# Graph attention with heads: exponentials and turnings run one chunk further ahead in tiles 5 to 23

## The chip, the cores and the metric

The kernel runs on one core of a Trainium2 chip. The core has five engines that run their own instruction streams and wait for each other by semaphores: TensorE (PE in the profile, with its weight loads as PEld), VectorE (DVE), ScalarE (ACT), GpSimd (POOL) and SyncE (SP), which in this kernel issues most of the DMA transfers. The metric is the device time of one execution in microseconds (us): the median of three runs for the kernel before, 2910.59 us.

## The reference

A network of two layers over 3327 nodes with 256 features. Layer 0 is a graph convolution and a mixture of 8 experts, layer 1 a graph attention and a block of four attention heads. The change lies in that last block alone, in the profile the stage from about 960 us to the end. Cut to it:

```python
sx = einsum('bsh,ndh->bnsd', layernorm(x), hl_w) + hl_b      # 4 heads of 64
q = einsum('bnsd,neod->bneso', sx, wq)                        # 4 query experts per head
k, v = einsum(sx, wk), einsum(sx, wv)
scores = einsum('bnesd,bntd->bnest', q, k) * 8 + causal
qkv = where(sx == 0, 0, softmax(scores) @ v)
gs = softmax(gate(qkv)); mixed = sum over the experts of qkv * gs
hn = layernorm(mixed + resid)                                 # resid from sx
out = x + gated(layernorm(fc2(relu(fc1(hn))) + hn))
```

So there are 3327 x 3327 causal scores for each of 16 pairs of head and query expert, each row with its own maximum, exponentials and sum, and then a weighted sum of values.

## The kernel before

Nodes are cut in 26 tiles of 128 rows. The method `heads` works through units, one for each tile t and head h, and cuts each unit's causal row of t + 1 key tiles into t // 4 + 1 chunks g of three or four key tiles (up to 512 columns). There are 392 chunks in all, 312 of them in tiles 5 to 23 (4 heads x 78). What happens to a chunk:

- `fill`: TensorE computes the scores of four query experts into four buffers of PSUM (pqk, 512 columns each), which are all that the pool `ps` has; other products use them too.
- `drain`: VectorE copies each of the four into SBUF (sc, one of nine buffers) and takes the row maximum on the way; the last chunk of a unit adds the causal mask, and then the maxima of the unit's chunks are reduced to anmax.
- `weigh`: ScalarE takes the exponentials in place, one instruction for each query expert, and their sums into aden. It needs anmax, so the unit must be fully drained.
- `turn`: VectorE transposes 32 x 32 blocks of sc in place.
- `values`: SyncE issues four transfers that bring the chunk's values into vr (three buffers).
- `attend`: TensorE multiplies the turned weights with vr into po, which collects over the chunks of a unit.

At a unit's end `over` takes po into ot times the mask sxd (ScalarE copies, GpSimd multiplies, from tile 5 on), and one step later `back` turns it with ptO into qkv. The generator `prepare` makes the projections of the next tile (psxt, pv, pk, pq) a part at a time, and `tail` mixes, normalises, applies the two linear layers and stores a finished tile; `run` advances them by one part, and `quiet` issues small exponentials that were put off.

The loop at the end of `heads` (from line 1493) sets the order of all of this by hand, and `InOrder` (lines 47 to 93) makes every engine keep the order in which its instructions are issued. Nearly all instructions therefore have line 61 in the profile, so groups are told apart by their tiles. One pass of the loop is a step. In step k the order was: drain as far as `wanted(k)`, value sums of chunk k, turning of chunk k + 1, value transfers and two exponentials of chunk k + 2, back and over where a unit has ended, parts of prepare and tail, the other exponentials of chunk k + 2, and the scores of one more chunk:

```python
drain_to(wanted(k))
attend(u, g)
if k + 1 < len(chunks):
    turn(*chunks[k + 1])
if ahead:                       # chunk k + 2
    values(*ahead)
    if ahead[1]:
        weigh(*ahead, range(2))
```

`wanted(k)` is k + 3 + t // 4 with t the tile of chunk k + 2: enough that the unit of that chunk is drained. In tiles 20 to 23 that keeps eight of the nine sc buffers in use, in tiles 24 and 25 all nine.

In tile 0 to 4 the queries of a tile (qts) lie in an sc buffer as well. `prepare` names its normalised features xn and its nonzero mask nz by one tag with one buffer, so the next tile's xn takes the buffer of this tile's nz. In tiles 0 to 4 two tiles can be in preparation at a time, four parts apart; later one is.

Of the kernel before, what the change touches and what calls it, by code (L numbers as in the profile page):

```python
# [12 lines left out]
F32 = mybir.dt.float32  # L13
# [9 lines left out]
P = 128  # L23
# [78 lines left out]
class Net:  # L102
# [753 lines left out]
    def heads(self, xs, vs, out):  # L856
        tc, a = self.tc, self.a
        nc = InOrder(tc)
        Q = 32
        with ExitStack() as ctx:  # L860
# [4 lines left out]
            tl = ctx.enter_context(tc.tile_pool(name="att", bufs=2))  # L865
            sm = ctx.enter_context(tc.tile_pool(name="atsm", bufs=4))
# [8 lines left out]


            load = dict(act=0.0, dve=0.0)
            lazy = deque()

            def empty(dst, src, n, scale=None):  # L880
                if load["act"] + 0.14 + 0.00086 * n <= load["dve"] + 0.1 + 0.00112 * n:
# [26 lines left out]
            def prepare(t, res):  # L908
# [43 lines left out]
                nz = self.work.tile([P, 2, P], F32, tag="xn", name="nz", bufs=1)  # L952
# [1 line left out]
                load["act"] += 0.6  # L954
                yield

                sxd = self.work.tile([P, 4, P], F32, tag="sxd", name="sxd", bufs=3)
                for k in range(2):
                    for s in range(2):
                        nc.sync.dma_start(  # L960
                            out=sxd[ds(64 * k, 64), s::2, :], in_=nz[ds(64 * s, 64), :, :]
                        )
                pp = ps.tile([P, 4, 64], F32, tag="b", name="pv")
                for c in range(2):
                    nc.tensor.matmul(
# [3 lines left out]
                empty(v, pp, D)  # L969
                yield  # L970

                pp = [ps.tile([P, 2, P], F32, tag="b", name="pk") for _ in range(2)]
                for c in range(2):
                    for s in range(2):
                        r = ds(64 * s, 64)
# [5 lines left out]
                for b in range(4):  # L981
                    nc.sync.dma_start(
                        out=vs[:, :, 4 * t + b, :].rearrange("h r d -> r h d"),
                        in_=v[ds(Q * b, Q), :, :],
# [9 lines left out]
                for c in range(2):  # L994
                    for i in range(2):
                        for s in range(2):
                            r = ds(64 * s, 64)
# [11 lines left out]
            def quiet():  # L1009

                while lazy:
                    lazy.popleft()()

            def run(gens):

                gens[:] = [g for g in gens if next(g, None) is None and g.gi_frame is not None]

            tails, preps, ready = [], [], {}
# [12 lines left out]
            def span(t, g):  # L1031


                n = t // 4 + 1
                lo, hi = (t + 1) * g // n, (t + 1) * (g + 1) // n
                return lo, hi - lo
# [42 lines left out]
            def weigh(u, g, experts):  # L1079

                n = span(u["t"], g)[1] * P
                q = ready[u["t"]]
                if u["h"] == g == 0 and 0 in experts:
                    q["den"] = sm.tile([P, 16, 7], F32, tag="den", name="aden", bufs=2)
                for k in experts:
                    e = u["sc"][g][:, k, :n]
                    nc.scalar.activation(
                        e, e, AF.Exp, bias=u["nmax"][:, k : k + 1],
                        accum_out=q["den"][:, 4 * u["h"] + k, g : g + 1],
                    )  # L1090
                    load["act"] += 0.26 + 0.00088 * n

            def values(u, g):

                lo, n = (4 * i for i in span(u["t"], g))
                v = u["v", g] = vrp.tile([P, 16, 64], F32, tag="vr", name="vr")
                for q in range(4):
                    nc.sync.dma_start(out=v[ds(Q * q, Q), :n, :], in_=vs[u["h"], :, lo : lo + n, :])

            def turn(u, g):  # L1100


                n = span(u["t"], g)[1] * P
                w = u["sc"][g][:, :, :n]
                nc.vector.transpose(w, w)
                load["dve"] += 0.1 + 0.00417 * n
# [7 lines left out]
            def attend(u, g):  # L1114


                t = u["t"]
                w, v = u["sc"][g], u["v", g]
                lo, n = (4 * i for i in span(t, g))
                for b2 in range(0, n, 2):  # L1120
                    for k in range(2):
                        for q in range(4):
                            r, b = ds(Q * q, Q), b2 + k

                            after = 4 * t + q - lo
                            if b > after and t:
                                continue
                            nc.tensor.matmul(
                                po[ds(64 * k, 64), q, :, :], v[r, b, :], w[r, :, ts(b, Q)],
                                start=(g == b2 == 0), stop=(b + 2 > after if t else b2 == 2),  # L1130
                            )

            def over(u):

                u["ot"] = tl.tile([P, 4, P], F32, tag="ot", name="ot", bufs=1)
                to = u["ot"].rearrange("p e (q i) -> p q e i", q=4)
                there = u["sxd"][:, u["h"] : u["h"] + 1, :]
                if u["t"] < 5 or u is units[-1]:

                    nc.vector.tensor_tensor(  # L1140
                        to, po,
                        there.rearrange("p o (q i) -> p q o i", q=4).to_broadcast([P, 4, 4, Q]),
                        ALU.mult,
                    )
                    load["dve"] += 0.7
                else:
                    nc.scalar.copy(to, po)
                    nc.gpsimd.tensor_tensor(
                        u["ot"], u["ot"], there.to_broadcast([P, 4, P]), ALU.mult
                    )  # L1150
                    load["act"] += 0.6
# [108 lines left out]
            def tail(t, sx, qkv, glp, den):  # L1260
# [35 lines left out]
                nz = tl.tile([P, 2, D], F32, tag="nzf", name="nzf", bufs=1)  # L1296
# [17 lines left out]
                fo = tl.tile([P, D], F32, tag="fo", name="fo", bufs=3)  # L1314
# [10 lines left out]
                fot = tl.tile([P, 2, P], F32, tag="fxt", name="fot", bufs=2)  # L1325
# [8 lines left out]
                f3 = fo.rearrange("p (h d) -> p h d", h=4)  # L1334
                nc.gpsimd.tensor_tensor(f3, f3, fg.unsqueeze(2).to_broadcast([P, 4, 64]), ALU.mult)
                nc.gpsimd.tensor_tensor(fo, fo, x, ALU.add)
                nc.sync.dma_start(out=out[ts(t, P), :], in_=fo)

            def last_tail(t, c, sx, r):

# [3 lines left out]
                if c == 0:  # L1344
                    r["fx"] = tl.tile([P, D], F32, tag="fx", name="fx", bufs=3)
                    r["fo"] = tl.tile([P, D], F32, tag="fo", name="fo", bufs=3)
                    r["fot"] = tl.tile([P, 2, P], F32, tag="fotl", name="fotl", bufs=1)
                else:
                    x = r["x"] = tl.tile([P, D], F32, tag="xend", name="xend", bufs=1)
                    nc.sync.dma_start(out=x, in_=xs[ts(t, P), :])  # L1350
                fx, fo, fot = r["fx"][:, half], r["fo"][:, half], r["fot"][:, c, :]
# [79 lines left out]
                fo, fot, x = r["fo"], r["fot"], r["x"]  # L1431
# [10 lines left out]
            chunks = [(u, g) for u in units for g in range(u["t"] // 4 + 1)]  # L1442
# [19 lines left out]
            def fill_next():  # L1462
                nonlocal filled
                if filled < len(chunks):
                    u, g = chunks[filled]
                    if g == 0:
                        begin(u)
                    fill(u, g)
                    filled += 1

            def drain_to(n):
                nonlocal drained
                while drained < min(n, len(chunks)):
                    if filled == drained:
                        fill_next()
                    drain(*chunks[drained])
                    drained += 1

            def wanted(k):

                return k + 3 + chunks[min(k + 2, len(chunks) - 1)][0]["t"] // 4

# [2 lines left out]
            for k in range(2):  # L1487
                values(*chunks[k])
                weigh(*chunks[k], range(4))
            turn(*chunks[0])  # L1490
            fill_next()
            ended = None
            for k, (u, g) in enumerate(chunks):
                ahead = chunks[k + 2] if k + 2 < len(chunks) else None
                drain_to(wanted(k))
                attend(u, g)
                if k + 1 < len(chunks):
                    turn(*chunks[k + 1])
                if ahead:
                    values(*ahead)  # L1500
                    if ahead[1]:
                        weigh(*ahead, range(2))
                if ended:
                    back(ended)
                last = u if g == u["t"] // 4 else None
                if last:
                    over(u)
                if not ended or u["t"] < 8:
                    run(preps)
                    run(tails)  # L1510
                ended = last
                if ahead:
                    weigh(*ahead, range(2 if ahead[1] else 0, 4))
                quiet()
                if filled == drained:
                    fill_next()
            back(ended)
            while tails:
                run(tails)
                quiet()  # L1520

# [552 lines left out]
```

## Time and profile before

| what | us |
|---|---|
| three runs | 2901.87, 2910.59, 2912.35 |
| the profiled execution: time, span | 2907.43, 2905.6 |
| mean granted TensorE clock over the span | 0.973 |
| busy: TensorE, VectorE, ScalarE, GpSimd | 2643.7, 2376.5, 1790.9, 1075.2 |
| turnings of tiles 0 to 4 (24 chunks) | 975 to 1117 |
| turnings of tiles 5 to 23 (312 chunks) | 1117 to 2633 |
| turnings of tiles 24 and 25 (56 chunks) | 2633 to 2876 |

The profile's page has an engine's busy time, the same in 40 equal slices of the span with a digit for tenths, the chain of work that ended last, and the groups of instructions by what they write and read (out<-in). A line of waits reads: the waiting engine and tile, the releasing engine and tile, us in total, times, longest. A row of a table by stretches gives the stretch and its length, then busy us and instructions of PE, PEld, DVE, ACT and POOL, the granted clock, the DMA share and GB/s. A row of a timeline gives the start, the duration, the engine, the operation, and in brackets how long the engine had been idle and what released it. "issue" is time in which an engine waited for nothing that the profile shows. Matmuls are pipelined and their ends are modelled.

### The profile page before, as it was taken

How to read it: one execution, taken by the hardware profiler on the slowest of the kernel's cores; microseconds unless marked ns; L12 is line 12 of the kernel's file. 1: busy time of each engine (PE TensorE's matmuls, PEld its weight loads, DVE VectorE, ACT ScalarE, POOL GpSimd, SP SyncE). 2: the span in 40 equal slices, each digit the busy share in tenths (PEclk: the TensorE clock that was granted, in tenths of full speed). 3: DMA queues.
4: the chain of work that ended last, by engine and by line, in shares of the span. 5: the costliest groups of instructions: out<-in, count | busy, mean ns of one | idle time of the engine just before them, and what ended most of it. 6: DMA issues, size and time to landing. Idle time of an engine off the chain costs nothing.

```text
span 2905.6 us, 125250 instructions
## 1 busy us (share of the span) xinstructions
PE 2643.7 (91%) x53422; PEld 1958.9 (67%) x53422; DVE 2376.5 (82%) x5525; ACT 1790.9 (62%) x5130; POOL 1075.2 (37%) x1562
## 2 busy tenths in 40 slices
PE   7999998779889799999999999999999999999995
PEld 5888888657668676666666666666666666556654
DVE  5203643689999597899999999999999999999996
ACT  6410145555545367777777776777667777677774
POOL 5541634622231148645454332333223222223122
PEclk9999989989999799999999999999999999999998
DMA  9994668647775233433434434343333433434332
GB/s 382 384 324 138 196 225 274 235 152 284 247 250 170 62 90 95 112 103 113 119 102 117 118 113 112 106 116 116 112 112 109 122 117 116 114 116 116 112 111 76
DMA packets 258189, 449.71 MB, mean 155 GB/s; under 512 B 58816, under 2 KB 156608, under 8 KB 257504
## 3 DMA queue, kind: packets, MB, share of 16 engines
q1 hardware_dynamic: 245536, 417.50, 45.9%
q0 software_dynamic: 6576, 18.02, 1.7%
q8 instruction: 421, 6.90, 1.0%
q10 hardware_dynamic: 5520, 6.18, 0.6%
q14 instruction: 136, 1.11, 0.1%
HBM read 393.37 MB, written 25.88 MB: 144 GB/s over the span
## 4 chain that ended last, share of the span: by engine, by line
DVE 34%; PE 28%; issue 3%; ACT 3%; POOL 1%; DMA 1%; SPq 0%; POOLq 0%; DVEq 0%; ACTq 0%
DVE sc L61 31%; PE po L61 11%; PE pqk L61 10%; PE ptO L61 2%; PE acc L61 2%; ACT sc L61 1%; PE psxt L61 1%; PE pq L61 1%; PE ph L61 1%; ACT sq L61 0%; PE pt L61 0%; DVE anmax L61 0%; POOL qkv L61 0%; SPq L61 0%; PE pk L61 0%
## 5 line engine op out<-in xcount | busy, mean ns | idle before, releaser
L61 ACT ACTIVATE sc<-sc,anmax 128x512 f32<-128x512 f32 (+3 forms) x1568 | 1041.4, 669 | 111.7 <-DVE anmax L61 111.7
L61 PEld LDWEIGHTS po<-sc,vr 32*64 32x64 f32 x43728 | 664.9, 131 | 390.6 <-DVE sc L61 232.9
L61 PE MATMUL po<-sc,vr 32*64 32x128 f32 x43728 | 770.6, 276 | 110.3 <-DVE sc L61 62.8
L61 DVE STREAM_TRANSPOSE sc<-sc 128x2048 f32<-128x2048 f32 (+3 forms) x392 | 816.2, 2082 | 10.7 <-ACT sc L61 10.4
L61 PE MATMUL pqk<-kt,qt 64*128 64x512 f32 (+1 forms) x2944 | 729.4, 585 | 14.7 <-DVE fgs L61 5.9
L61 DVE TENSOR_SCALAR_CACHE_REDUCE sc<-pqk 128x512 f32<-128x512 f32 (+2 forms) x1152 | 654.7, 622 | 64.3 <-PE pqk L61 63.0
L61 PEld LDWEIGHTS pqk<-kt,qt 64*128 64x128 f32 x2944 | 290.5, 187 | 224.5 <-issue 107.3
L61 PE MATMUL acc<-wh,p 128*128 128x259 f32 x1352 | 310.0, 387 | 35.0 <-DVE p L61 34.8
L61 PEld LDWEIGHTS acc<-wh,p 128*128 128x128 f32 x1352 | 254.2, 191 | 93.1 <-DVE p L61 52.5
L61 PE MATMUL acc<-y,pan 128*128 128x256 f32 x1352 | 298.2, 382 | 1.7 <-issue 1.7
L61 ACT ACTIVATION_READ_ACCUMULATOR sc<-sc,anmax 128x1 f32 x1568 | 299.3, 191 | 0.0
L61 PEld LDWEIGHTS acc<-y,pan 128*128 128x128 f32 x1352 | 257.1, 191 | 37.9 <-issue 2.5
L61 POOL TENSOR_TENSOR ot<-ot,sxd 128x512 f32<-128x512 f32 x83 | 106.0, 1277 | 474.7 <-ACT ot L61 460.9
L61 DVE CUSTOM_DVE_ANT_0 sc<-pqk,mask 128x512 f32<-128x512 f32 (+3 forms) x416 | 242.2, 637 | 28.6 <-PE pqk L61 27.7
L61 ACT ACTIVATE u<-u,d 128x512 f32<-128x512 f32 (+1 forms) x182 | 125.2, 688 | 159.8 <-DVE u L61 159.7
L61 DVE SCALAR_TENSOR_TENSOR u<-bc,d 128x512 f32<-128x512 f32 (+1 forms) x182 | 135.7, 746 | 0.1
L61 DVE SCALAR_TENSOR_TENSOR p<-pan,u 128x512 f32<-128x512 f32 (+1 forms) x182 | 126.8, 697 | 10.2 <-PE acc L61 5.8
L61 ACT COPY qkv<-ptO 128x272 f32<-128x272 f32 x104 | 39.7, 382 | 143.9 <-PE ptO L61 143.9
L61 PE MATMUL ptO<-igw,ot 128*128 128x68 f32 x832 | 116.1, 283 | 1.9 <-DVE mx L61 0.8
L61 ACT ACTIVATE junk<-ar 128x1664 bf16<-128x1664 f32 x52 | 82.8, 1592 | 55.7 <-DMA ar<-in_adj_dram 55.2
L61 PEld LDWEIGHTS ptO<-igw,ot 128*128 128x128 f32 x832 | 101.5, 192 | 20.0 <-issue 12.7
L61 DVE CUSTOM_DVE_ANT_0 sg<-sg,dst 128x1664 bf16<-128x1664 bf16 (+2 forms) x56 | 99.7, 1789 | 1.2 <-ACT dst L61 1.0
(356 smaller groups left out, 3086.6 us busy)
## 6 DMA issues: line engine op xcount, KB each, us to landing
vr<-vs SPq DMA_DIRECT2D x976, 128.0 KB
ar<-in_adj_dram SPq DMA_DIRECT2D x104, 832.0 KB
vr<-vs SPq DMA_DIRECT2D x544, 96.0 KB
pan<-in_adjt_dram SPq DMA_DIRECT2D x156, 256.0 KB
pan<-in_adjt_dram SPq DMA_DIRECT2D x26, 1024.0 KB
pan<-in_adjt_dram SPq DMA_DIRECT2D x20, 832.0 KB
w1e<-w SPq DMA_DIRECT2D x59, 256.0 KB
took<-places SPq DMA_DIRECT2D x59, 129.0 KB
```

Of the source, the lines that this page charges most:

```text
L61: made = make(*args, **kw)
```

## The change

The exponentials of a chunk and its turning are issued one step earlier while chunk k belongs to tile 5 or later and chunk k + 3 to tile 23 or earlier (`extra(k)` is then 1): exponentials for chunk k + 3, turning for chunk k + 2, and `wanted(k)` drains one chunk further. Two counters, `flipped` and `weighed`, replace the fixed distances. Value transfers stay two chunks ahead. The two exponentials ahead of `back` and `over` and the rest behind the parts of prepare and tail keep their places in the step.

The store of a finished tile is put in a list, and `quiet` issues it at the end of the second step after it was listed. The four transfers of sxd move behind the value projection, one part of `prepare` later. aden has a third buffer, and fotl of the last tile uses the two buffers of xres in place of its own.

```diff
@@ prepare: the mask transfers after the value projection
+                pp = ps.tile([P, 4, 64], F32, tag="b", name="pv")
+                for c in range(2):
+                    nc.tensor.matmul(
+                        pp[:, 2 * c : 2 * c + 2, :], sxt[:, c, :], wv[:, c, :], start=True, stop=True
+                    )
+                v = self.work.tile([P, 4, 64], F32, tag="v", name="v", bufs=1)
+                empty(v, pp, D)
+                yield
+
                 sxd = self.work.tile([P, 4, P], F32, tag="sxd", name="sxd", bufs=3)
                 for k in range(2):
                     for s in range(2):
                         nc.sync.dma_start(
                             out=sxd[ds(64 * k, 64), s::2, :], in_=nz[ds(64 * s, 64), :, :]
                         )
-                pp = ps.tile([P, 4, 64], F32, tag="b", name="pv")
...
-                empty(v, pp, D)
-                yield
@@ quiet
                 while lazy:
                     lazy.popleft()()
+                for store in stores:
+                    store[0] -= 1
+                while stores and stores[0][0] < 0:
+                    stores.popleft()[1]()
@@ weigh
-                    q["den"] = sm.tile([P, 16, 7], F32, tag="den", name="aden", bufs=2)
+                    q["den"] = sm.tile([P, 16, 7], F32, tag="den", name="aden", bufs=3)
@@ tail
-                nc.sync.dma_start(out=out[ts(t, P), :], in_=fo)
+                stores.append([2, partial(nc.sync.dma_start, out=out[ts(t, P), :], in_=fo)])
@@ last_tail
-                    r["fot"] = tl.tile([P, 2, P], F32, tag="fotl", name="fotl", bufs=1)
+                    r["fot"] = tl.tile([P, 2, P], F32, tag="xres", name="fotl", bufs=2)
@@ the loop
+            def extra(k):
+
+                t = chunks[min(k + 3, len(chunks) - 1)][0]["t"]
+                return int(chunks[k][0]["t"] >= 5 and t // 4 + 1 <= 6)
+
             def wanted(k):
 
-                return k + 3 + chunks[min(k + 2, len(chunks) - 1)][0]["t"] // 4
+                c = min(k + 2 + extra(k), len(chunks) - 1)
+                return k + 3 + extra(k) + chunks[c][0]["t"] // 4
...
-            ended = None
+            ended, flipped, weighed = None, 1, 2
             for k, (u, g) in enumerate(chunks):
-                ahead = chunks[k + 2] if k + 2 < len(chunks) else None
                 drain_to(wanted(k))
                 attend(u, g)
-                if k + 1 < len(chunks):
-                    turn(*chunks[k + 1])
-                if ahead:
-                    values(*ahead)
-                    if ahead[1]:
-                        weigh(*ahead, range(2))
+                while flipped < min(k + 2 + extra(k), weighed, len(chunks)):
+                    turn(*chunks[flipped])
+                    flipped += 1
+                if k + 2 < len(chunks):
+                    values(*chunks[k + 2])
+                rest = []
+                while weighed < min(k + 3 + extra(k), len(chunks)):
+                    c = chunks[weighed]
+                    if c[1]:
+                        weigh(*c, range(2))
+                    rest.append((*c, range(2 if c[1] else 0, 4)))
+                    weighed += 1
                 if ended:
                     back(ended)
...
-                if ahead:
-                    weigh(*ahead, range(2 if ahead[1] else 0, 4))
+                for c in rest:
+                    weigh(*c)
                 quiet()
...
-            while tails:
+            while tails or stores:
                 run(tails)
                 quiet()
```

More of the change, by code (lines that the diff above doesn't have):

```diff
@@ L877, in heads @@
             load = dict(act=0.0, dve=0.0)
-            lazy = deque()
+            lazy, stores = deque(), deque()
             def empty(dst, src, n, scale=None):
@@ L955, in prepare @@
                 yield
[L957 to L962, printed above, removed]
                 pp = ps.tile([P, 4, 64], F32, tag="b", name="pv")
@@ L970, in prepare @@
                 yield
+                sxd = self.work.tile([P, 4, P], F32, tag="sxd", name="sxd", bufs=3)
+                for k in range(2):
+                    for s in range(2):
+                        nc.sync.dma_start(
+                            out=sxd[ds(64 * k, 64), s::2, :], in_=nz[ds(64 * s, 64), :, :]
+                        )
                 pp = [ps.tile([P, 2, P], F32, tag="b", name="pk") for _ in range(2)]
```

## The prediction

> **What bounds the kernel now.** I read the page's parts 1, 2 and 4 first, to see which engines fill the stage that the change touches, then the table by stretches, then the waits of each engine in that stage, and last a timeline of one stall.
>
> ```profile
> PE 2643.7 (91%) x53422; PEld 1958.9 (67%) x53422; DVE 2376.5 (82%) x5525; ACT 1790.9 (62%) x5130; POOL 1075.2 (37%) x1562
> ...
> DVE  5203643689999597899999999999999999999996
> ...
> DVE 34%; PE 28%; issue 3%; ACT 3%; POOL 1%; DMA 1%; SPq 0%; POOLq 0%; DVEq 0%; ACTq 0%
> DVE sc L61 31%; PE po L61 11%; PE pqk L61 10%; PE ptO L61 2%; PE acc L61 2%; ACT sc L61 1%; PE psxt L61 1%; PE pq L61 1%; PE ph L61 1%; ACT sq L61 0%; PE pt L61 0%; DVE anmax L61 0%; POOL qkv L61 0%; SPq L61 0%; PE pk L61 0%
> ```
>
> The 392 turnings (the transposes of sc, in chunk order) date the chunks: tile 5 is turned from 1117 us, tile 24 from 2633 us, and what lies between, 1516 us, is where the change works. Its 312 chunks take 4.86 us each. The table by stretches and the waits of VectorE, TensorE and SyncE's queue, each asked for 1117 to 2633 us (engine <- releaser: us, times, longest):
>
> ```profile
> 1117.00:2633.00 1516.00, 1420.61 (x39861) 968.75 (x39851) 1426.45 (x3205) 1101.89 (x3471) 567.91 (x778) 0.99 0.39 113
> ```
> ```profile
> DVE sc L61 <- PE pqk L61: 74.6, 89, 4.4
> ...
> DVE sc L61 <- ACT sc L61: 1.4, 3, 1.0
> ...
> PE po L61 <- DVE sc L61: 42.9, 61, 1.5
> PE po L61 <- issue: 29.9, 35, 1.8
> ...
> SPq L61 <- PE po L61: 572.6, 247, 6.6
> SPq L61 <- POOL fo L61: 115.0, 20, 8.8
> ...
> SPq L61 <- POOL nz L61: 7.4, 7, 1.3
> ```
>
> VectorE and TensorE are each busy 94% here and take turns on the chain. VectorE idles 89.5 us, 74.6 of them waiting for scores. TensorE idles 95 us, 42.9 of them at the head of a value sum, for the turning. A timeline of both engines shows the two waits as one event:
>
> ```profile
> 1628.44 2.30 DVE L61 STREAM_TRANSPOSE sc<-sc 128x2048 f32<-128x2048 f32 x1
> ...
> 1632.56 1.77 DVE L61 STREAM_TRANSPOSE sc<-sc 128x1536 f32<-128x1536 f32 x1
> 1634.79 0.69 DVE L61 TENSOR_SCALAR_CACHE_REDUCE sc<-pqk 128x512 f32<-128x512 f32 x1 [0.46 <-PE pqk L61]
> ...
> 1627.64 1.65 PE L61 MATMUL pqk<-kt,qt 64*128 64x384 f32 x8
> 1630.80 2.09 PE L61 MATMUL po<-sc,vr 32*64 32x128 f32 x116 [1.51 <-DVE sc L61]
> 1632.82 0.44 PE L61 MATMUL pt<-ident,xn 128*128 128x128 f32 x2
> 1633.09 0.61 PE L61 MATMUL ph<-fc,h 128*128 128x128 f32 x4
> 1633.63 1.99 PE L61 MATMUL pqk<-kt,qt 64*128 64x512 f32 x8
> ```
>
> TensorE stood 1.51 us until the turning of this very chunk ended, then had a value sum, 0.81 us of other work and the next scores to do, and VectorE, through with its second turning, found none and stood 0.46 us. Had the value sum begun 0.46 us sooner, VectorE would not have stood.
>
> **The change, part by part.**
>
> Work per step: nothing added or removed. A chunk keeps four drains (0.61 us apart at 512 columns), one turning (2.24 us), four exponentials and the same matmuls. Draining, exponentials and turning all move one chunk further ahead of the value sum, so their spacing among themselves stays: exponentials one step before their turning, as now. Only the value sum's gate loosens: chunk k was turned one step before, now two.
>
> What that is worth. Removing TensorE's waits gains only where VectorE's stalls follow them. By stretch (1117 to 1363, to 1632, to 1980, to 2289, to 2633 us) VectorE waits for scores 22.0, 10.7, 17.0, 15.4, 9.5 us and TensorE for turnings 1.9, 6.0, 10.5, 9.1, 15.3 us. No stretch can give more than the smaller of its two: 1.9 + 6.0 + 10.5 + 9.1 + 9.5 = 37.0 us. And TensorE cannot save up at will: scores fill four banks, the last of which is free only when the previous drain ends; the second half of a fill (1.0 of 1.99 us) follows, and the turning takes 2.24 us, so a value sum can begin at most some 1.2 us before that turning ends. Going through the stalls in order, crediting each with the TensorE waits since the last one, carrying no more than 1.0 us, gives 16 us; with 1.5 us, 19; the 37 needs no limit. The row nearest to a typical stall (1.51 us waited, 0.46 stalled) is paid in full, so it lies above the 16 and 19; many stalls follow a run in which TensorE is full, so it lies well under the 37. I take 24 us and keep both ends. The first stretch gives almost nothing: TensorE is full there. Late next after that: still the scores, behind TensorE's own extra work (1.1 us of ptO, 1.16 of psxt).
>
> A page of the Trainium skill judges this otherwise. Perfetto Trace Analysis, Identifying the Most-Contended Engine, holds matmul busy time a bad measure of how full TensorE is, and weight-load busy time a good one. By it TensorE, at 968.75 of 1516 us, has a third to spare, and the whole 74.6 us would go; the timeline above, where each matmul group from 1630.80 on starts when the one before is due to end, does not agree.
>
> Entry and exit. At chunk 24 one extra fill and drain stand ahead of the value sum and four more exponentials behind it, at chunk 25 there is a second turning; at chunk 333 there is no drain and no turning. VectorE's total is unchanged; it waits once for the first bank pair of the extra fill (about 1 us, half of 1.99) and once for a value sum at the exit (up to 2.09, or nothing where TensorE has a lead). Bounds 0 to 4 us, I take 2, the middle.
>
> Score buffers: in tiles 20 to 23 all nine instead of eight are live. The new drain needs the buffer of the value sum before last, and its scores come after that sum in TensorE's order, so it waits no longer than for its scores. Cover: tiles 24 and 25 run with nine now, and VectorE waits for scores only 3.5 us from 2633 to 2758 us. Cost 0.
>
> Stores: 22 here, 0.357 us of issue each, unchanged in number. Now SyncE's queue stands 115.0 us behind POOL's last addition into fo, with the four vr transfers of the next chunk behind it, and TensorE waits for those. It waited 4.0 us for vr in all, 8 times. Issued two steps (some 10 us) later the store waits for nothing; fo has three copies, one taken per tile of 43 us or more. Gain 0 to 4 us; I take 1, since the waits seen sit mostly in the shadow of the scores before them.
>
> Mask transfers: four of 0.606 us per tile, past one chunk's vr transfers and value projection, in front of the same vs stores. SyncE loses a 7.4 us wait for POOL's nz. From tile 5 on they are read a tile later. In tiles 1 to 4 the next tile's normalising takes the buffer of nz, so POOL waits for the transfer: 3.8 us, once, now. One step there is 147 us / 24 = 6.1 us, three tiles: 0 to 18 us. VectorE idles 37 of those 147 us, which covers part of it, and the one wait seen is 3.8 us, far from the upper end: I take 1.
>
> The third aden copy and fotl in the xres buffers: no instruction; xres was last loaded a tile earlier. Cost 0.
>
> Sum: -24 + 2 - 1 + 1 = -22 us. The profiled execution took 2907.4 us (span 2905.6 and 1.8 around it), 3.2 us under the median 2910.6; so 2885 us, 0.9% under the median.
>
> **Rivals.**
>
> 1. TensorE is simply full. Its 29.9 us of issue gaps and its back-to-back groups stay, stalls are paid a step later, under 10 us is left: about 2902 us. For: the first stretch, 22.0 us of stalls with 1.9 of waits. Against: the last, where the waits exceed the stalls.
>
> 2. Slower, by ScalarE. In tiles 8 to 11 (three chunks a head) the exponentials of a head's first chunk now fall in the step that also copies ptO, and the copy stands ahead of them; ScalarE waited for ptO 36.7 us in 18 waits from 1117 to 1363 us, 2.0 each, up to 4.1. VectorE then stands before the turning. The slack is a turning and a drain less four exponentials: 1.7 + 1.9 - 2.4 = 1.2 us at 384 columns, 1.9 at 512; from a copy later than that on, it decides. Its price is 16 heads by 2.0 us, 32 us, and with the lead eaten up by it the time is 2907.4 + 32 = 2939 us; at half the price, with the gain kept, 2901. Against: tiles 5 to 7 have this order now, and VectorE waits for exponentials 1.4 us in the whole stretch.
>
> 3. VectorE alone bounds it: all 74.6 us go, 2907.4 - 74.6 = 2833 us. For: VectorE's digits of 9 in slices 18 to 39. Against: the stretch sums above. The page named above sides with this one.
>
> **The numbers.** Forecast 0.60, rival 1 0.18, rival 2 0.14, rival 3 0.08. Forecast's own range: -37 - 4 to -16 + 4 + 7, so 2866 to 2902 us. The range of 2855 to 2918 us takes that in with the runs' own spread (2901.9 to 2912.4), all of rival 1 and the mild part of rival 2; beyond it lie most of rival 3 and the rest of rival 2, under 2 in 10. Half a percent, 14.6 us, is about what a measurement of this kernel can tell from no change: under 2896 us counts as faster. That is 0.88 of the forecast and rival 3: 0.61. Slower: rival 2 and a little of the rest, 0.16. Same: 0.23.
>
> **What would show it.** Right: "PE po <- DVE sc" falls from 42.9 us to under 10, "DVE sc <- PE pqk" from 74.6 to about 50; "SPq <- POOL fo" is gone; the turnings of tiles 5 to 23 span about 1494 us; the stretch to 1363 us hardly moves. Rival 1: the first wait falls and the second stays. Rival 2: "DVE sc <- ACT sc" grows from 1.4 us to 15 or more, in tiles 8 to 11. Rival 3: "DVE sc <- PE pqk" falls under 15. I would be wrong if TensorE's waits merely change name (to "PE pqk <- DVE sc", the banks), if its clock drops below the 0.99 of this stretch when it is pressed harder, or if tiles 0 to 4 lengthen beyond 147 us.

## The result and the profile after

| | before | changed |
|---|---|---|
| median, us | 2910.59 (2901.87 to 2913.4) | 2867.09 (2863.63 to 2868.76) |
| profiled execution: span, us | 2905.6 | 2862.2 |
| first turning of the stage, us | 974.8 | 982.1 |
| turnings of tiles 0 to 4, us | 142.2 | 141.8 |
| turnings of tiles 5 to 23, us | 1516.2 | 1468.3 |
| turnings of tiles 24 and 25, us | 242.6 | 240.5 |

The ratio is 0.9848 (95% interval 0.9834 to 0.9863): 1.5% faster, where 0.9% was forecast. The gain lies where the change works: 47.9 us in tiles 5 to 23. The first turning came 7.4 us later in this execution; 7.0 us of that lay ahead of the stage's first projection (psxt), in stages that the change does not touch. The page of the changed kernel, parts 1, 2 and 4:

```profile
PE 2665.0 (93%) x53422; PEld 1979.1 (69%) x53422; DVE 2368.9 (83%) x5525; ACT 1790.0 (63%) x5130; POOL 1075.3 (38%) x1562
...
DVE  5203643589999588899999999999999999999996
...
DVE 35%; PE 28%; ACT 3%; issue 2%; POOL 1%; DMA 0%; SPq 0%; POOLq 0%; DVEq 0%; ACTq 0%
```

The same five engines, tiles 5 to 23 (from 1124 to 2592 us here), in the table by stretches:

```profile
1124.00:2592.30 1468.30, 1443.59 (x39850) 991.73 (x39841) 1420.80 (x3205) 1102.96 (x3474) 568.06 (x779) 1.00 0.40 116
```

The waits of VectorE, TensorE and SyncE's queue in the same stretch (us, times, longest):

```profile
DVE sc L61 <- PE pqk L61: 34.5, 36, 4.5
DVE sc L61 <- ACT sc L61: 0.6, 2, 0.4
...
PE pqk L61 <- DVE sc L61: 4.9, 6, 2.0
PE po L61 <- issue: 2.2, 4, 1.3
...
PEld pqk L61 <- DVE sc L61: 53.8, 201, 2.6
...
SPq L61 <- POOL fo L61: 5.8, 4, 2.6
```

The line "PE po <- DVE sc" (42.9 us before) is gone; a little of it came back as "PE pqk <- DVE sc", the wait for a bank of scores (2.1 before, 4.9 now), and the weight loads of a fill wait longer for a bank ("PEld pqk <- DVE sc", 26.5 us before, 53.8 now). VectorE's wait for scores fell by 40.1 us, from 89 waits to 36. Of the forecast's signs, "SPq <- POOL fo" did not quite go: 5.8 us are left. VectorE is busy 96.8% of the stretch (94.1% before), TensorE 98.3% by its modelled ends. One thing in these lines was not forecast: TensorE's idle time inside the value sums that the profile ascribes to nothing, "PE po <- issue", fell from 29.9 us to 2.2.

The two engines in the timeline of the changed kernel, to be held against the one in the prediction:

```profile
2023.42 2.31 DVE L61 STREAM_TRANSPOSE sc<-sc 128x2048 f32<-128x2048 f32 x1
2025.65 0.65 DVE L61 CUSTOM_DVE_ANT_0 sc<-pqk,mask 128x512 f32<-128x512 f32 x1
...
2022.61 2.32 PE L61 MATMUL pqk<-kt,qt 64*128 64x512 f32 x8
2023.56 0.54 PEld L61 LDWEIGHTS pqk<-kt,qt 64*128 64x128 f32 x4 [0.32 <-DVE sc L61]
2024.86 2.10 PE L61 MATMUL po<-sc,vr 32*64 32x128 f32 x128
2026.89 0.71 PE L61 MATMUL ph<-fxt,fc 128*128 128x128 f32 x4
2027.53 2.05 PE L61 MATMUL pqk<-kt,qt 64*128 64x512 f32 x8
```

The value sum starts at 2024.86 us, 0.79 us before VectorE is through with the turning and takes its next instruction, at 2025.65; under the old order it would have waited for that end. In the whole of tiles 5 to 23 about half of the value sums start before the turning at the place of the old gate ends, by up to 1.46 us; before the change none did. The fill ahead of this one took 2.32 instead of 1.99 us: its second half stood 0.32 us for a bank, in the row of the weight loads (PEld).

### The profile page after: what moved, and what is told of

Same layout as the page of the kernel before. It is cut to its first block, busy times and chain, and to the rows that moved or that the text cites. A ratio compares the mean times of both kernels' runs of the same rounds, so it can differ in the third digit from the quotient of the medians.

```text
span 2862.2 us, 125012 instructions
## 1 busy us (share of the span) xinstructions
PE 2665.0 (93%) x53422; PEld 1979.1 (69%) x53422; DVE 2368.9 (83%) x5525; ACT 1790.0 (63%) x5130; POOL 1075.3 (38%) x1562
## 4 chain that ended last, share of the span: by engine, by line
DVE 35%; PE 28%; ACT 3%; issue 2%; POOL 1%; DMA 0%; SPq 0%; POOLq 0%; DVEq 0%; ACTq 0%
DVE sc L61 32%; PE pqk L61 10%; PE po L61 10%; PE acc L61 2%; ACT sc L61 2%; PE ptO L61 2%; PE psxt L61 1%; PE pt L61 1%; PE pq L61 1%; PE ph L61 0%; ACT sq L61 0%; PE pk L61 0%; PE pv L61 0%; DVE anmax L61 0%; DVE gl L61 0%
## 5 line engine op out<-in xcount | busy, mean ns | idle before, releaser
L61 PE MATMUL po<-sc,vr 32*64 32x128 f32 x43728 | 761.1, 276 | 31.6 <-DVE sc L61 21.5
L61 PE MATMUL pqk<-kt,qt 64*128 64x512 f32 (+1 forms) x2944 | 764.4, 585 | 19.0 <-DVE fgs L61 6.6
L61 PEld LDWEIGHTS pqk<-kt,qt 64*128 64x128 f32 x2944 | 315.9, 185 | 239.5 <-issue 80.9
```

The source lines that it names most:

```text
L61: made = make(*args, **kw)
```

## Experiments

### Which part of the change it is

Theory L: the lead alone is the gain. Theory S: since the issue gaps went too, and SyncE's queue no longer stands behind POOL, the stores are part of it. Three kernels, each with one part:

```diff
 lead_only, against the changed kernel (and sxd back in front of pv)
-                stores.append([2, partial(nc.sync.dma_start, out=out[ts(t, P), :], in_=fo)])
+                nc.sync.dma_start(out=out[ts(t, P), :], in_=fo)
 stores_only (sxd back too), masks_only (store back too)
-                return int(chunks[k][0]["t"] >= 5 and t // 4 + 1 <= 6)
+                return 0
```

> The lead of draining, exponentials and turning as in the changed kernel; the store is issued at once and the mask transfers stand in front of the value projection, as before. Theory L (the lead alone is the gain): ratio to the kernel before 0.985 to 0.987, TensorE's waits for turnings at the head of a value sum in tiles 5 to 23 near 0 and its issue gaps in value sums near 2 us, as in the changed kernel. Theory S (the 29.9 us of issue gaps went because SyncE's queue no longer stands behind POOL): ratio 0.991 to 0.994, the issue gaps still 20 to 30 us.

> Only the stores are issued later; no lead, mask transfers as before. Theory L: ratio 0.999 to 1.001, issue gaps in value sums near 30 us. Theory S: ratio 0.992 to 0.995, issue gaps under 10 us. In both the queue's waits behind POOL's fo fall from 115 us to under 10.

> Only the mask transfers are issued one part of the preparation later; no lead, stores as before. By the prediction's term: 0 to +18 us, taken as 1, so a ratio of 1.000 to 1.002, with tiles 0 to 4 lasting 142 to 145 us between turnings. If the move lengthens the start: ratio up to 1.006. If it frees the queue for the value transfers: 0.998.

| | median, us | before, us | ratio, 95% interval |
|---|---|---|---|
| lead_only | 2862.50 | 2905.97 | 0.9848 (0.9835 to 0.986) |
| stores_only | 2906.02 | 2905.97 | 1.0002 (0.999 to 1.0015) |
| masks_only | 2911.55 | 2905.97 | 1.0013 (1.0 to 1.0026) |

The lead alone is the whole gain. In stores_only the queue's wait behind fo fell to 20.6 us (more than the under 10 expected) and the issue gaps stayed at 26.6 us: Theory S falls. Of lead_only, where the queue still stands, TensorE's and the queue's waits:

```profile
PE po L61 <- issue: 4.9, 7, 1.4
...
SPq L61 <- POOL fo L61: 104.0, 17, 10.6
```

So the gaps went with the lead. The masks cost 0.13%, some 4 us, at the edge of what can be told from nothing; tiles 0 to 4 lasted 142.7 us there, and POOL's wait for sxd at the start became 6.4 us in two waits in the changed kernel, 3.8 in one before.

### Which of the three that move

> The changed kernel, but each chunk is turned one step ahead of its value sum as before; draining and exponentials keep their extra chunk, stores and masks as changed. Theory L with the turning as its gate: ratio to the kernel before 0.998 to 1.002, and the waits for turnings at the head of value sums back at 40 us or more. Rival (the gain comes from draining and exponentials being further ahead, or from the queue): ratio 0.985 to 0.990.

```diff
-                while flipped < min(k + 2 + extra(k), weighed, len(chunks)):
+                while flipped < min(k + 2, weighed, len(chunks)):
```

Measured: 2889.00 us, ratio 0.994 (0.9927 to 0.9954). Neither side had this: with the old gate back (38.0 us of waits for turnings) two fifths of the gain (0.6 of 1.5%) are still there. The next run takes the exponentials back too:

> The changed kernel with draining one chunk further ahead only; exponentials two chunks and turning one chunk ahead as before. With the turning kept at one chunk the last run still gained 17 us (ratio 0.994). Theory E (exponentials being early is that gain, since VectorE and what waits for ScalarE no longer meet them): ratio 0.999 to 1.001 here. Theory D (the drain's place is the gain: scores and drain of another chunk than the turned one): ratio 0.993 to 0.995. Theory C (only the place of the code moved): anywhere from 0.993 to 1.003, with the issue gaps in value sums in other tiles than before.

```diff
-                while weighed < min(k + 3 + extra(k), len(chunks)):
+                while weighed < min(k + 3, len(chunks)):
```

Measured: 2905.04 us against 2911.29, ratio 0.9982 (0.997 to 0.9994). So of the 1.5%, taken back in this order, draining one chunk further gives about 0.2, the exponentials 0.4 and the turning 0.9; another order was not tried. TensorE's and VectorE's waits, drain_ahead_only first, then turning_one_ahead:

```profile
PE po L61 <- DVE sc L61: 39.9, 72, 1.5
PE po L61 <- issue: 28.7, 37, 1.3
...
DVE sc L61 <- PE pqk L61: 67.5, 80, 5.7
```
```profile
DVE sc L61 <- PE pqk L61: 54.2, 66, 4.1
...
PE po L61 <- DVE sc L61: 38.0, 70, 1.5
PE po L61 <- issue: 20.7, 28, 1.5
```

The gate stays equal (39.9 and 38.0) while stalls and issue gaps both shrink as the exponentials move. Theory C is not excluded: 0.9982 lies in its wide range, and some of the gaps are in other tiles than before. Theory E is closest otherwise, though 0.9982 lies below its 0.999, and its reason, that VectorE meets fewer late exponentials, is not in the trace: "DVE sc <- ACT sc" was 1.4 us to begin with. Why the exponentials' place takes 13 us off the stalls stays open. What the pair shows about the turning is plain: only without the gate do the issue gaps go (28 gaps with it, 4 without).

### Whether a longer lead is worth more

> The changed kernel with a lead of two chunks in tiles 5 to 19 and of one in tiles 20 to 23. The prediction held that four banks of scores let a value sum start at most 1.2 us before the old gate, so that a longer lead is worth nothing: ratio to the kernel before 0.984 to 0.986, as the changed kernel. Rival (TensorE can save up more): ratio under 0.981, stalls for scores under 20 us.

```diff
-                t = chunks[min(k + 3, len(chunks) - 1)][0]["t"]
-                return int(chunks[k][0]["t"] >= 5 and t // 4 + 1 <= 6)
+                s, t = (chunks[min(k + i, len(chunks) - 1)][0]["t"] for i in (4, 3))
+                if chunks[k][0]["t"] < 5:
+                    return 0
+                return 2 if s // 4 + 1 <= 5 else int(t // 4 + 1 <= 6)
```

Measured: 2870.22 us, ratio 0.9861 (0.9842 to 0.9881), the changed kernel's within the intervals; VectorE's wait for scores in tiles 5 to 23 (1123.8 to 2597.2 us):

```profile
DVE sc L61 <- PE pqk L61: 38.0, 45, 6.3
```

A second chunk brings nothing: with one, no value sum waited for its turning any more. The traces bear out the banks' limit too. In tiles 5 to 19 a value sum starts at most 1.45 us before the turning at the place of the old gate ends, with a lead of one at most 1.46, and in both 95% start under 1.1 us before it; the 1.2 of the prediction was a little low. No matmul of a value sum waited for vr in tiles 5 to 23 of either run, so the value transfers, which stayed two chunks ahead, were not the limit.

### How full TensorE is

> The changed kernel, but the four matmuls of ptO are issued twice in tiles 5 to 23: 76 units by 1.04 us, 79 us of work for TensorE that changes no result. Theory F (TensorE is full in these tiles): the time grows by 50 to 80 us, ratio to the kernel before 1.002 to 1.013, and VectorE's waits for scores grow from 35 us to 90 or more. Theory H (TensorE has about a third to spare, as its weight loads' busy share says): the time grows by under 15 us, ratio 0.985 to 0.990.

```diff
-                for e in range(4):
+                for e in 2 * list(range(4)) if 5 <= u["t"] <= 23 else range(4):
                     nc.tensor.matmul(
                         pt[:, e, :], u["ot"][:, e, :], igw[:, h, e, :], start=True, stop=True
                     )
```

Measured: 2904.37 us, ratio 0.9973 (0.996 to 0.9987): 0.0125 above the changed kernel, 36 us for 79 us of work, and VectorE's waits for scores grew from 34.5 to 67.5 us, not to 90. Neither theory. The tables by stretches, tiles 5 to 13 and 14 to 23, of the changed kernel and of this one:

```profile
1124.00:1628.40 504.40, 493.52 (x12715) 346.13 (x12700) 474.01 (x1165) 379.85 (x1202) 267.91 (x365) 0.99 0.38 112
1628.40:2592.30 963.90, 950.07 (x27137) 645.59 (x27141) 946.78 (x2043) 723.11 (x2274) 300.15 (x414) 1.00 0.41 119
```
```profile
1126.50:1654.80 528.30, 518.30 (x12992) 374.13 (x12976) 476.37 (x1165) 378.96 (x1199) 267.81 (x365) 0.99 0.37 107
1654.80:2634.00 979.20, 969.23 (x27455) 668.90 (x27458) 948.43 (x2043) 724.49 (x2278) 300.21 (x414) 1.00 0.40 117
```

In tiles 5 to 13, 36 units add 37.4 us of work and 23.9 us of time (64%); in tiles 14 to 23, 40 units add 41.6 us and 15.3 (37%). TensorE bounds the early tiles more, VectorE, busy 98% of the second stretch, the late ones. A matmul busy share of 98% was not full, and weight loads at 67% did not mean a third to spare: the rule of the Trainium skill's Perfetto Trace Analysis (Identifying the Most-Contended Engine), that weight-load share tells TensorE's room better, was off here on its side as the matmul share was on the other.

### Where the issue gaps come from

Theory C: a gap arises where TensorE's instructions pass a multiple of 256 within a value sum. Three successive gaps in the timeline of the kernel before:

```profile
2036.63 2.00 PE L61 MATMUL po<-sc,vr 32*64 32x128 f32 x119
2039.47 0.45 PE L61 MATMUL po<-sc,vr 32*64 32x128 f32 x9 [0.84 <-issue]
2039.85 0.44 PE L61 MATMUL pt<-ident,fx 128*128 128x128 f32 x2
2040.22 1.99 PE L61 MATMUL pqk<-kt,qt 64*128 64x512 f32 x8
2042.14 1.84 PE L61 MATMUL po<-sc,vr 32*64 32x128 f32 x109
2044.50 0.65 PE L61 MATMUL po<-sc,vr 32*64 32x128 f32 x19 [0.52 <-issue]
2045.08 0.71 PE L61 MATMUL ph<-fxt,fc 128*128 128x128 f32 x4
2045.72 1.99 PE L61 MATMUL pqk<-kt,qt 64*128 64x512 f32 x8
2047.64 1.65 PE L61 MATMUL po<-sc,vr 32*64 32x128 f32 x96
2049.79 0.70 PE L61 MATMUL po<-sc,vr 32*64 32x128 f32 x32 [0.50 <-issue]
```

From gap to gap it is 9 + 2 + 8 + 109 = 128 and 19 + 4 + 8 + 96 = 127 matmuls, each with its weight load: 256 and 254 instructions. With the semaphore instructions of TensorE's sequencer, which the rows leave out, the count is exact: of the 35 gaps in the kernel before, 32 stand at the same place, 193 or 194 past a multiple of 256, counted over all of TensorE's instructions in the trace. Three kernels shift the code at the start of the stage (N is 64, then 32):

```diff
             kt = one.tile([P, 4, NP], F32, name="kt")
+            pad = ps.tile([P, 4], F32, tag="b", name="pad")
+            for _ in range(N):
+                nc.tensor.matmul(pad, self.ident, fgw[:, 0, :], start=True, stop=True)
```

> The kernel before with 64 matmuls of 128x4 added at the start of the stage, where TensorE waits for the first tile: TensorE's later instructions lie 128 places, half of 256, further on. Theory C (the issue gaps lie where TensorE's code passes a multiple of 256 instructions, and which passages stand depends on what falls there): gaps in other places of the value sums, 64 matmuls off, their sum between 15 and 45 us, the time 2890 to 2925 us. Rival (the gaps belong to the data or the transfers): same places, same sum within 4 us, time within 5 us of before plus at most 9 us for the added matmuls.

This run told nothing apart, by a slip of mine: each such matmul became two records with two weight loads, so that 64 shift the code by 256 instructions, which changes no place within the 256. They took 25.3 us, and the run 2931.07 us, ratio 1.0069 (1.0049 to 1.0088). It does show that the gaps recur: tile 7 at 6 us, tile 15 at 10, 16 and 22, tile 17 at 11 and 21, as in two other executions without the lead. Half as many:

> The kernel before with 32 matmuls of 128x4 added at the start of the stage. The trace of the run with 64 showed 128 matmul records and as many weight loads, 256 instructions, 25.3 us: a shift by a whole 256, which left the gaps where they were. 32 make 128 instructions and 12.7 us, up to 13 us later at the first turning. Theory C (a gap arises where TensorE's code passes a multiple of 256 instructions inside a value sum): the gaps of tile 7 at 5.8 us, tile 15 at 10 to 23 us, tile 17 at 11 us and tile 23 at 63 to 73 us, which three runs shared, go, and others of the same kind come in other tiles; their sum is between 10 and 50 us, and the stretch of tiles 5 to 23 may take 1490 to 1530 us. Rival (they belong to data, transfers or the order of the work): the same tiles and times as before.

> The changed kernel with the same 32 matmuls at the start of the stage. If the lead takes the gaps away wherever the code's passages fall: issue gaps in value sums under 7 us, tiles 5 to 23 within 4 us of the 1468 us of the changed kernel, and the ratio to the kernel before 0.985 to 0.990 with the up to 13 us at the start. If the changed kernel merely happened on a good place: gaps of 15 us or more, tiles 5 to 23 at 1480 us or more, ratio over 0.993.

| | issue gaps in value sums, us (number) | tiles 5 to 23, us | ratio, 95% interval |
|---|---|---|---|
| before | 29.9 (35) | 1516.2 | 1 |
| before_half_shift | 18.4 (25) | 1500.4 | 0.9983 (0.9967 to 1.0) |
| changed | 2.2 (4) | 1468.3 | 0.9848 (0.9834 to 0.9863) |
| after_half_shift | 3.7 (4) | 1473.8 | 0.9872 (0.9854 to 0.989) |

Shifted by 128, the gaps of tiles 7 (at 6 us), 17 and 23 (at 63 to 73 us) are gone, those of tile 15 lie at 37 to 48 us, and new ones came in tiles 14, 19 and 20. Only three stayed, of another kind: they stand ahead of a whole value sum, in tiles 10, 11 and 22. Theory C holds. With the lead there are few gaps on either place (tiles 5 to 23 came out 5.5 us longer, a little over the 4 allowed); the changed kernel did not just land well. Counted over all instructions, the gaps of the three shifted kernels and the 4 of the changed one stand at 193 or 194 past a multiple of 256 again, but for the three of the other kind.

What TensorE stands for there is in the traces too. One DMA queue moves instructions in packets of 16,384 bytes, and in each of the twelve runs their number is that of TensorE's instructions divided by 256, rounded down: 107881 / 256 = 421.4 and 421 packets before, 107645 / 256 = 420.5 and 420 in the changed kernel. Taken in order, one packet belongs to each passage. Of the 313 passages in tiles 5 to 23 of the kernel before, the 32 with a gap have TensorE going on 1.2 to 1.6 us after their packet has landed, and that packet had started only 2.2 to 3.2 us ahead; at the others it started 3.8 us ahead in the median. So the engine stands for its next instructions, whose transfer began late. With the lead the late ones are rare: a tenth of the packets began 2.4 us or more after the passage before theirs in the kernel before, 1.2 us or more in the changed one.

## Why the prediction was right, and where it was short

The mechanism was right as far as it went: the value sum's gate was the turning, its waits went from 42.9 us to none, and VectorE's stalls for scores fell in their place. The time, 2867 us, lies in the forecast's own range, at its lower edge, and that is in part luck: by the count below, about half of the fall in stalls came by a way that the prediction had held fixed. The term that was mis-sized is the lead: 24 us, with "no stretch can give more than the smaller of its two", 37 us. Measured: stalls down 40.1 us, the stretch down 47.9.

- The rule that credits stalls with the waits before them gave 16 to 19 us, and a part of that size came. The stalls that follow no issue gap fell from some 52 to 34.5 us, by about 18 (a stall counts as following one up to the gap's length, where the gap lies less than 9 us ahead of it).
- The rest of the stalls, some 22 us (21 to 24 as one pairs them), did follow issue gaps, and went to 0 with them. This split is a way of counting; no run separates the two parts. I had put those 29.9 us of gaps down as TensorE's own and fixed; this is the step that failed. For the same reason the stretch bound did not hold: the first stretch saved 6.1 us of stalls where its waits for turnings were 1.9, and it shortened by 8.6 us where I said it would hardly move.
- Another 7.8 us of the stretch were no stalls for scores: VectorE was busy 5.7 us less and idle 2.1 us less otherwise. Their cause is open.
- The banks' limit of some 1.2 us was nearly right: 1.46 us at most, and a lead of two chunks gave no more.
- Score buffers: nine in use cost nothing, stalls in tiles 21 to 23 fell from 9.5 to 1.8 us. Stores, taken as 1 us of gain: 0.05 us between the medians, nothing that can be told. Masks, taken as 1 us: up to 4 us alone, within the bounds. Entry and exit, 2 us, can't be told apart in the trace.
- Rival 1 (TensorE simply full) falls: the stalls halved. Rival 2 (ScalarE) falls: "DVE sc <- ACT sc" is 0.6 us. Rival 3 (all stalls go) was too much: 34.5 us are left, 15.9 of them in tiles 5 to 9.
- Two slips in the working: the 7 us at the range's upper end is none of its terms (the masks' own bound, 18, would have made it 2913), and the 147 us of tiles 0 to 4 start at 970 us; from the first turning it was 142.2. Neither touches the forecast of 2885.
- The stretch was to span 1494 us and the stalls to be about 50: 1468 and 34.5.

## What to carry to other kernels

Where two engines each wait a little for the other in every step and both are over 90% busy, try the gate between them one step further ahead. The waits that lie ahead of stalls gave about half of the gain here, and a lead beyond what the banks let through was worth nothing. Idle time that a profile ascribes to nothing need not be fixed: find out at which places in the code it recurs, and whether it still does when the engine no longer stands at that gate. And before a shift of code is used as a test, count the instructions that it really adds.

## What the runs showed of the hardware

TensorE can stand 0.2 to 1.8 us where its instructions pass from one block of 256 to the next, in the kernel before at 32 of the 313 passages in tiles 5 to 23 for 28.3 us, and another engine stands behind it. The instruction queue's packets in this trace have 16,384 bytes (421 in the kernel before), which is 64 bytes for each of 256. The Trainium skill's Runtime: NRT & Kernel Launch (Instruction fetch mechanics) has code come in blocks of 256 instructions, the crossing "mostly hidden": the 256 agrees, and so does "mostly" (281 of 313), but what was not hidden counted. Why transfers begin late behind a gate at the head of the value sums, and not with the lead, was not tried and stays open.

Shifting the kernel before by half a block moved tiles 5 to 23 from 1516.2 to 1500.4 us, in one execution each; the medians agree, 5.4 us lower though the added matmuls took some 12 us. Executions of the kernel before spread from 2897.3 to 2912.5 us beside lead_only's 2861.6 to 2863.5. With the gate, it seems, small differences in time decide at which passages TensorE stands; that is argued, not tested.
